# Projections of a cross-attention in a fixed order of TensorE, with a split first load and two products of zeros ahead

## The chip, the core and the metric

The kernel runs on one core of a Trainium2 chip. The core has a matrix engine (TensorE, PE in the profile; its weight loads are listed as PEld), a vector engine (VectorE, DVE), an engine for activations (ScalarE, ACT), GpSimd (POOL), and SyncE (SP), whose queue issues nearly all DMAs of this kernel. Work is held in SBUF, products come out in PSUM (eight banks), inputs, outputs and stored intermediates lie in DRAM. The metric is the time of one execution on the device in microseconds (us); three runs of the kernel before gave a median of 2944.82.

## What is computed

Two blocks of a gated network on x (8 batches, 512 rows, 256 columns). The change touches the first part of the first block, a cross-attention of x with a context, with 16 heads of 64:

```python
q = layernorm(x) @ Wq.T + bq          # 512 x 1024 for each batch
k = ctx @ Wk.T + bk
v = ctx @ Wv.T + bv
gate = relu(box_embedding(boxes) @ Wg.T + bg)      # 512 x 512 for each head
att = softmax(log(max(gate, 1e-6)) + q k.T / sqrt(64))
x1 = x + tanh(g_xattn) * (att v @ Wo.T + bo)
```

The kernel takes the gate, with its floor of 1e-6, as a factor on exp of the scores. After it come an attention over the batch, a mixture of eight experts, a second cross-attention and a spiking feed-forward layer, which stay as they are. All is 32-bit floating point.

## The kernel before, in words

`gated_cross_attention` (L273) has two stages. The **projection stage** (L371 to L406) computes keys, values and queries of all eight batches, stores them to DRAM (`kdr`, `vdr`, `qdr` in the profile), and prepares the terms of the gate from the boxes. The **attention stage** (from L408) reads them back, for 32 blocks of 128 queries.

*The projections* (`project_all`, L177). The setup loads the bias `bk`, four pieces of the key weights `wk_` (256 KB each), and after the first piece batch 0's context `ctxT` (512 KB) and rows `xt` (512 KB); then `wv`, `bv`, `wq`, `bq`. VectorE scales `wq` and `bq` (L209, L210). `batch(b)` (L215) issues the loads of batch b+1, takes the statistics of `xt` (L60 to L63, in `Ctx.stats`; the power -0.5 is on GpSimd) and normalizes it in place (L68). Then come eight key tiles: `project` (L223) makes each as two 128x512 products over the two halves c of the 256 columns into a PSUM tile `pk`, and ScalarE adds the bias and writes it to an SBUF tile `st` (L230), which a DMA stores (L235). Each product shows as two PE instructions in the profile, so a tile is four. Eight value tiles follow in the same way into `pv`; VectorE adds the bias into `vs` (L245), stored once per batch (L251). Then `xt` is transposed by PE into `pt` and copied to `xnT` (L258, L261), and eight query tiles are made with `project` and stored (L264). PSUM has two buffers each of `pk`, `pv` and `pt`; `st` has four buffers, and a fifth tile waits until the store of the first has landed.

*The boxes* (`box_terms`, L85). At setup, key centres `kcs` are computed from a load `kc` and stored (L98 to L102, `kcd<-kcs`); sizes are turned into sines and cosines `tt` on ScalarE (L105 to L126); `tt` is put in another order (`tk`), transposed by PE in two pieces through one PSUM tile, copied to `tT` and stored (L129 to L140, `kxd<-tT`). Its `batch(b)` makes and stores `asb` (L154 to L172). In batches 1 to 5, `offsets` and `features` (L399 to L406) prepare the gate's inputs `emb` of the first query blocks on VectorE and ScalarE, with pieces of some 1.5 to 2.8 us each.

*Who sets the order.* In the projection stage nothing is fixed by hand: a planner (part of the language's compiler) puts the instructions of every engine, and the DMA issues of SP, in an order. It takes what it believes ready, the earlier in the code first. Every engine and SP's queue then run their lists strictly in that order. In the attention stage, PE, ScalarE and VectorE follow the order of the code (`manual_schedule`, L561), except for the first block's gate products (L557 to L560), which the planner places.

*The boundary.* The pools of the attention stage, `xbig` (gate tiles), `xwk` (loads, scores) and `xps` (PSUM), lie where the released pools of the projection stage lay. By default, whatever first uses such memory waits for all users of the released pools there. Its first instructions are the loads of `qT`, `kT` and `v` (L430, L419, L425), 20 gate halves (L449, copied by ScalarE and VectorE in turn, L455) and the first scores (L469).

*Before all this*, L1696 to L1699 load the two gates of the network into `tg` and take their Tanh.

Of the kernel before, what the change touches and what calls it, by code (L numbers as in the profile page):

```python
# [12 lines left out]
F32 = mybir.dt.float32  # L13
I32 = mybir.dt.int32
AF = mybir.ActivationFunctionType
ALU = mybir.AluOpType
# [4 lines left out]
P = 128  # L21
# [63 lines left out]
def box_terms(cx, a, d, es):  # L85
# [40 lines left out]
    )  # L126


    tk = wk.tile([P, 2, 8, NT // 2], F32, name="tk")  # L129
    for g in range(2):  # L130
        nc.vector.tensor_copy(
            tk[:, g], tt[:, g * NT // 2 : (g + 1) * NT // 2].rearrange("p t a c -> p (a c) t")
        )
        pt = ps.tile([P, P], F32, name="pt", tag="t")
        nc.tensor.transpose(pt, tk[:, g].rearrange("p j t -> p (j t)"), ident)
        tT = w2.tile([P, P], F32, name="tT", tag="tT")
        nc.vector.tensor_copy(tT, pt)
        nc.sync.dma_start(
            out=d["kx"][g, 0:8, :].rearrange("j (t p) -> (j t) p", p=P), in_=tT
        )  # L140
    one = wk.tile([B // 2, S], F32, name="one")
    nc.gpsimd.memset(one, 1.0)
    for g in range(2):
# [7 lines left out]
    neg = wm[:, 0, :, H : 2 * H]  # L151
    nc.vector.tensor_scalar(neg, neg, -1.0, None, ALU.mult)

    def batch(b):  # L154

        shape = [P, NQ, 4, 2 * H]
        parts = []
        for c in range(2):
            part = w2.tile(shape, F32, name=f"asb{c}", tag=f"asb{c}")
            nc.vector.tensor_tensor(  # L160
                part, wm[:, c].unsqueeze(1).to_broadcast(shape),
                tt[:, b * NQ : (b + 1) * NQ, :, c].unsqueeze(3).to_broadcast(shape), ALU.mult,
            )
            parts.append(part)
        asb = parts[0]
        nc.vector.tensor_tensor(asb, asb, parts[1], ALU.add)
        for t in range(NQ):
            r0 = (b * NQ + t) * P
            nc.sync.dma_start(
                out=d["qx"][:, r0 : r0 + P, :].rearrange("j p h -> p j h"),  # L170
                in_=asb[:, t].rearrange("p a (c h) -> p (a c) h", h=H),
            )  # L172
# [1 line left out]
    return batch  # L174


def project_all(cx, a, d, wp):  # L177

    tc, nc, ident = cx.tc, cx.nc, cx.ident
    wk = wp.enter_context(tc.tile_pool(name="qw", bufs=1))  # L180
# [1 line left out]
    ps = wp.enter_context(tc.tile_pool(name="qps", bufs=2, space=PSUM))  # L182
    ctxTs, xts = {}, {}

    def load(b):
        ctxTs[b] = w2.tile([P, 2, S], F32, name="ctxT", tag="ctxT")
        nc.sync.dma_start(out=ctxTs[b], in_=a["ctxT"][b])
        xts[b] = w2.tile([P, NQ, D], F32, name="xt", tag="xt")
        nc.sync.dma_start(
            out=xts[b], in_=a["x"][b * S : (b + 1) * S, :].rearrange("(t p) d -> p t d", p=P)  # L190
        )

    wk_ = wk.tile([P, 2, H * DK], F32, name="wk_")
    bk = wk.tile([P, PAIRS], F32, name="bk")
    nc.sync.dma_start(out=bk, in_=a["bk"])
    for m in range(4):
        cols = slice(m * 2 * P, (m + 1) * 2 * P)
        nc.sync.dma_start(out=wk_[:, :, cols], in_=a["wkT"][:, :, cols])
        if m == 0:
            load(0)  # L200
    wv = wk.tile([P, 2, H * DK], F32, name="wv")
    nc.sync.dma_start(out=wv, in_=a["wvT"])
    bv = cx.bcast(wk, a["bv"], "bv")
# [8 lines left out]
    for v in vs:  # L212
        nc.gpsimd.memset(v[:, :, :, :, DK : DK + 1], 1.0)

    def batch(b):  # L215
        if b + 1 < B:
            load(b + 1)
        ctxT, xt = ctxTs.pop(b), xts.pop(b)
        mv, rs = cx.stats(w2, xt, NQ)
        xn = xt  # L220
        cx.normalize(xn, xt, mv, rs, NQ)

        def project(w, bias, src, name, m):  # L223
            pk = ps.tile([P, S], F32, name="pk", tag="p")
            for c in range(2):
                nc.tensor.matmul(  # L226
                    pk, w[:, c, m * P : (m + 1) * P], src[:, c, :], start=(c == 0), stop=(c == 1)
                )
            st = w2.tile([P, S], F32, name="st", tag="st", bufs=4)
            nc.scalar.activation(st, pk, AF.Identity, bias=bias[:, m : m + 1])  # L230
            return st

        for m in range(PAIRS):
            st = project(wk_, bk, ctxT, "k", m)
            nc.sync.dma_start(out=d["k"][b, m], in_=st)  # L235
        v = vs[b % 2]
        for kc in range(NQ):
            for n in range(2):
                pv = ps.tile([P, 512], F32, name="pv", tag="v")
                for c in range(2):  # L240
                    nc.tensor.matmul(  # L241
                        pv, ctxT[:, c, kc * P : (kc + 1) * P], wv[:, c, n * 512 : (n + 1) * 512],
                        start=(c == 0), stop=(c == 1),
                    )
                nc.vector.tensor_tensor(  # L245
                    v[:, 4 * n : 4 * n + 4, kc, :, 0:DK],
                    pv.rearrange("p (a t d) -> p a t d", t=2, d=DK),
                    bv[:, n * 512 : (n + 1) * 512].rearrange("p (a t d) -> p a t d", t=2, d=DK),
                    ALU.add,
                )  # L250
        nc.sync.dma_start(  # L251
            out=d["v"][b].rearrange("a p k -> p a k"), in_=v.rearrange("p a k t d -> p a (k t d)")
        )
        xnT = w2.tile([P, 2, S], F32, name="xnT", tag="xnT")
        for c in range(2):
            pt = ps.tile([P, S], F32, name="pt", tag="t")
            for t in range(NQ):
                nc.tensor.transpose(  # L258
                    pt[:, t * P : (t + 1) * P], xn[:, t, c * P : (c + 1) * P], ident
                )  # L260
            nc.vector.tensor_copy(xnT[:, c, :], pt)  # L261
        for m in range(PAIRS):
            st = project(wq, bq, xnT, "q", m)
            nc.sync.dma_start(  # L264
                out=d["q"][b * NQ : (b + 1) * NQ, :, m, :].rearrange("t p q -> p t q"),
                in_=st.rearrange("p (t q) -> p t q", q=P),
            )
        return xnT

    return batch  # L270


def gated_cross_attention(cx, a, tg, x1q, d, front):  # L273

# [3 lines left out]
    with ExitStack() as es:  # L280
# [16 lines left out]
        def load_keys(b):  # L297
            for r0 in (0, 2 * QB, 64, 64 + 2 * QB):
                nc.sync.dma_start(
                    out=kd[r0 : r0 + 2 * QB, b % 2, :],  # L300
                    in_=d["kc"][2 * b + (1 if r0 % 64 else 0)].partition_broadcast(2 * QB),
                )
# [63 lines left out]
        def features(j, *fns):  # L366
            for fn in fns:
                if 0 <= j < NSTEP:
                    fn(j)

        with ExitStack() as pro:  # L371
            batch = project_all(cx, a, d, pro)
            bp = pro.enter_context(tc.tile_pool(name="bq", bufs=1))
            box = box_terms(cx, a, d, pro)
            bx = bp.tile([P, NSTEP * NP, 2], F32, name="bx")
# [4 lines left out]
            nc.vector.tensor_tensor(qi, bx[:, :, 1], bx[:, :, 0], ALU.subtract)  # L380
            nc.vector.tensor_scalar(qi, qi, 1.0, None, ALU.add)
            nc.vector.reciprocal(qi, qi)
            for b in range(B):
                xnT = batch(b)
                box(b)
                if b == 0:
                    load_keys(0)

                if b < 4:
                    w, cols = wst[b // 2], slice(b % 2 * 8 * P, (b % 2 + 1) * 8 * P)  # L390
                    nc.gpsimd.tensor_copy(w[0:1, cols][:, 0:1], xnT[0:1, 0, 0:1])
                    nc.sync.dma_start(out=w[0:GR, cols], in_=a["wst"][:, cols])
                if b in (4, 5):
                    w = wo[:, 4 * (b - 4) : 4 * (b - 3), :]
                    nc.gpsimd.tensor_copy(w[0:1, 0, 0:1], xnT[0:1, 0, 0:1])
                    nc.sync.dma_start(out=w, in_=a["woT"][:, 4 * (b - 4) : 4 * (b - 3), :])
                if b == 6:
                    bo = cx.bcast(cp, a["bo"], "bo")
                if b in (1, 3, 5):  # L399
                    j = b // 2  # L400
                    offsets(j, 0, NP)
                    features(j, sizes, clip, log)
                if b in (2, 4):
                    j = b // 2 - 1
                    load_products(j)
                    features(j, turns, whole, rest, rest_sizes, sines, place)  # L406

        front(-1)  # L408
        big = es.enter_context(tc.tile_pool(name="xbig", bufs=2))
        wk = es.enter_context(tc.tile_pool(name="xwk", bufs=2))  # L410
        ps = es.enter_context(tc.tile_pool(name="xps", bufs=1, space=PSUM))
        gates, qTs, xts, kTs, vTs = {}, {}, {}, {}, {}
        es_, ats, pos, oTs = {}, {}, {}, {}

# [1273 lines left out]
def flamingo_gated_block(ctx: ExitStack, tc: tile.TileContext, a, out):  # L1688
# [4 lines left out]


    tg = const.tile([P, 5], F32, name="tg")
    nc.sync.dma_start(out=tg[:, 0:2], in_=a["g_xattn"].partition_broadcast(P))  # L1696
    nc.sync.dma_start(out=tg[:, 2:4], in_=a["g_ffn"].partition_broadcast(P))
    nc.scalar.activation(tg[:, 0:4], tg[:, 0:4], AF.Tanh)
    nc.vector.tensor_scalar(tg[:, 4:5], tg[:, 3:4], 0.2, None, ALU.mult)  # L1699

    x1q = [dram.tile([B * P, D], F32, name=f"x1q{q}") for q in range(NQ)]
    y1d = dram.tile([NT * P, D], F32, name="y1d")
# [33 lines left out]
            j = slice(2 * k - 10, 2 * k - 8)  # L1736
            cx.normalize(xf0[:, j], xf0[:, j], mv[:, j], rs[:, j], 2)

    gated_cross_attention(cx, a, tg, x1q, d, front)

    lp = ctx.enter_context(tc.tile_pool(name="late", bufs=1))
    moe = ctx.enter_context(tc.tile_pool(name="moe", bufs=1))
# [146 lines left out]
```

## Time and profile before

| what | value |
|---|---|
| runs of the kernel before | 2944.82 us median (2941.93 to 2946.64) |
| the profiled execution | 2944.38 us, its span 2942.6 us |
| PE busy over the span | 2887.5 us (98%), 15308 matmul instructions |
| DVE, ACT, POOL busy | 1826.0, 1411.9, 138.6 us |
| first PE instruction | 7.52 us |
| last projection product | run of 32 query instructions from 340.06 us |
| first gate product (L449) | 354.90 us |
| first scores (L469) | 363.02 us |
| 7.52 to 363.00 us | PE busy 347.69, DVE 126.74, ACT 121.86 of 355.48 us; DMA share 0.70 |

How to read it: the span runs from the first to the last instruction of the execution. A timeline row gives the start, the duration, the engine, the line of the code, the output and the inputs, the number of instructions merged in it, and in brackets how long the engine had been idle before it and what ended the wait. "SPq" rows are DMA issues on SP's queue. Matmuls are pipelined and their ends are modelled, so PE is read by the starts of its instructions and by its idle times rather than by its busy share.

### The profile page before, as it was taken

What the parts mean: (1) busy time and instruction counts of PE and PEld (TensorE: products, weight loads), DVE (VectorE), ACT (ScalarE), POOL (GpSimd) and SP (SyncE); (2) the same over time, 40 slices, a digit from 0 to 9 for tenths busy, and PEclk for the clock granted to TensorE, in tenths of its full rate; (3) what the DMA queues carried; (4) which work ended last, traced back from release to release, by engine and by line L of the source; (5) the groups of instructions that cost most, each with busy time, mean ns of one, the idle gap of its engine ahead of it and who ended that gap; (6) DMA issues with size and microseconds to landing.
All of it is one profiled execution on the core that took longest, in us unless ns stands there. A gap on an engine that the chain in (4) does not pass through costs nothing.

```text
span 2942.6 us, 39447 instructions
## 1 busy us (share of the span) xinstructions
PE 2887.5 (98%) x15308; PEld 2114.9 (72%) x15308; DVE 1826.0 (62%) x2862; ACT 1411.9 (48%) x2212; POOL 138.6 (5%) x138
## 2 busy tenths in 40 slices
PE   8999999999999999999999999999999999999998
PEld 3444478888888888888888888877776666456566
DVE  6432177777777777777777778557862012566758
ACT  4332256566666666656565665425542112343434
POOL 2000000000000000000000000000002111212100
PEclk9999999999999999999999999999999999999999
DMA  7775545555555555554646464543124432211000
GB/s 226 220 232 182 180 119 154 143 153 144 148 154 143 156 141 159 135 163 131 166 133 168 128 166 129 138 135 129 49 58 138 149 127 93 93 43 58 29 15 22
DMA packets 269338, 386.05 MB, mean 131 GB/s; under 512 B 55304, under 2 KB 133000, under 8 KB 266336
## 3 DMA queue, kind: packets, MB, share of 16 engines
q1 hardware_dynamic: 266080, 375.15, 44.0%
q0 software_dynamic: 3072, 8.39, 1.0%
q8 instruction: 121, 1.98, 0.3%
q14 instruction: 65, 0.53, 0.1%
HBM read 237.23 MB, written 78.07 MB: 107 GB/s over the span
## 4 chain that ended last, share of the span: by engine, by line
PE 79%; DVE 13%; DMA 2%; issue 2%; ACT 1%; SPq 1%; POOL 0%; ACTq 0%; DVEq 0%; POOLq 0%
PE pg L449 13%; PE po L505 11%; PE pS L469 7%; PE pk L226 6%; PE pT L485 6%; PE ph L1535 4%; PE pw L536 4%; PE ph L1320 4%; PE py L1329 4%; PE py L1550 4%; PE pv L241 3%; DVE nm L473 2%; PE pz L1507 2%; DVE lt L346 2%; PE pq L700 2%
## 5 line engine op out<-in xcount | busy, mean ns | idle before, releaser
L476 ACT ACTIVATE e<-pS,nm 128x512 f32<-128x512 f32 x512 | 323.8, 683 | 577.7 <-DVE nm L473 577.1
L449 PE MATMUL pg<-wst,emb 116*128 116x208 f32 (+1 forms) x2560 | 582.5, 351 | 8.1 <-DVE gate L455 5.8
L449 PEld LDWEIGHTS pg<-wst,emb 116*128 116x128 f32 x2560 | 414.7, 190 | 205.9 <-issue 81.2
L505 PEld LDWEIGHTS po<-v,at 128*128 128x128 f32 x4096 | 493.0, 192 | 0.1
L505 PE MATMUL po<-v,at 128*128 128x65 f32 x4096 | 485.7, 272 | 0.0
L473 DVE TENSOR_REDUCE nm<-pS 128x2 f32<-128x1024 f32 x256 | 312.6, 1221 | 176.4 <-PE pS L469 176.4
L487 DVE SCALAR_TENSOR_TENSOR at<-gate,pT 128x1024 f32<-128x1024 f32 x256 | 311.2, 1215 | 47.1 <-PE pT L485 46.1
L469 PE MATMUL pS<-kT,qT 64*128 64x512 f32 x1024 | 292.3, 643 | 5.1 <-ACT e L476 2.0
L485 PE MATMUL pT<-ident,e 128*128 128x128 f32 x2048 | 266.5, 273 | 0.0
L485 PEld LDWEIGHTS pT<-ident,e 128*128 128x128 f32 x2048 | 239.8, 141 | 14.0 <-DVE o L513 1.5
L455 DVE COPY gate<-pg 128x416 f32<-128x416 f32 (+1 forms) x289 | 164.7, 570 | 51.4 <-PE pg L449 31.1
L455 ACT COPY gate<-pg 128x416 f32<-128x416 f32 x351 | 166.5, 530 | 34.1 <-PE pg L449 31.7
L1333 DVE TENSOR_TENSOR ye<-py,b 128x256 f32<-128x256 f32 x32 | 13.6, 424 | 208.0 <-PE py L1329 208.0
L1324 ACT ACTIVATE hT<-ph,eb 128x512 f32<-128x512 f32 x64 | 44.0, 687 | 174.9 <-PE ph L1320 174.9
L226 PE MATMUL pk<-ctxT,wk__129 128*128 128x512 f32 x256 | 114.8, 604 | 10.3 <-DMA ctxT<-in_ctxT 7.5
L63 POOL TENSOR_TENSOR ln_rs<-ln_ve,mhalf 128x4 f32<-128x4 f32 (+1 forms) x25 | 25.4, 1017 | 2049.4 <-DVE ln_ve L62 1989.2
L1535 PE MATMUL ph<-xnT,wf 128*128 128x512 f32 (+2 forms) x320 | 118.7, 513 | 1.8 <-ACT xnT L1405 1.8
L536 PE MATMUL pw<-wo,oT 128*128 128x256 f32 x512 | 117.6, 383 | 0.5 <-ACT oT L528 0.5
L241 PE MATMUL pv<-wv,ctxT 128*128 128x512 f32 x256 | 114.7, 594 | 1.2 <-DVE vs L245 1.1
L469 PEld LDWEIGHTS pS<-kT,qT 64*128 64x128 f32 x1024 | 78.2, 185 | 50.5 <-issue 36.5
L1320 PE MATMUL ph<-dT,w 128*128 128x512 f32 x256 | 111.9, 595 | 2.4 <-DVE dT L1305 2.4
L226 PE MATMUL pk<-xnT,wq 128*128 128x512 f32 x256 | 112.8, 594 | 0.6 <-DVE xnT L261 0.6
(259 smaller groups left out, 3959.8 us busy)
## 6 DMA issues: line engine op xcount, KB each, us to landing
v<-vdr SPq DMA_DIRECT2D x256, 260.0 KB
kT<-kdr SPq DMA_DIRECT2D x256, 256.0 KB
emb<-lt SPq DMA_DIRECT2D x64, 520.0 KB
emb<-nt SPq DMA_DIRECT2D x64, 520.0 KB
vdr<-vs SPq DMA_DIRECT2D x8, 2080.0 KB
kdr<-st SPq DMA_DIRECT2D x64, 256.0 KB
qdr<-st SPq DMA_DIRECT2D x64, 256.0 KB
qT<-qdr SPq DMA_DIRECT2D x32, 512.0 KB
```

Of the source, the lines that this page charges most:

```text
L226: nc.tensor.matmul(pk, w[:, c, m * P : (m + 1) * P], src[:, c, :], start=(c == 0), stop=(c == 1))
L449: nc.tensor.matmul(pg[:, c, 0 : nq * H], embs[i % 2][R, blk // 2, blk % 2, kc * P : (kc + 1) * P], wst[i % 2][R, q0 * H : (q0 + nq) * H], ...
L455: copy(gates[i][:, :, 2 * hf : 2 * hf + 2, q0 : q0 + nq].rearrange("p h k q -> p k h q"), pg[:, :, 0 : nq * H].rearrange("p k (q h) -> p k ...
L469: nc.tensor.matmul(pS[:, t, :], qTs[i][rows, p, :], kT[rows, :], start=True, stop=True)
L473: nc.vector.tensor_reduce(nm, pS, AX.X, ALU.max, negate=True)
L476: nc.scalar.activation(e[:, t, :], pS[:, t, :], AF.Exp, bias=nm[:, t : t + 1])
L485: nc.tensor.transpose(pT[:, t, kc, :], e[:, t, kc * P : (kc + 1) * P], ident)
L487: nc.vector.scalar_tensor_tensor(at, gates[i][:, 2 * p : 2 * p + 2], 1e-6, pT, ALU.max, ALU.mult)
L505: nc.tensor.matmul(po[:, 2 * (p % 2) + t, :], at[:, t, kc, :], v[:, kc, t, :], start=(kc == 0), stop=(kc == NQ - 1),)
L536: nc.tensor.matmul(pw, oT[:, c, :], wo[:, c, :], start=(c == 0), stop=(c == PAIRS - 1))
L1320: nc.tensor.matmul(ph, w1[:, c, f * P : (f + 1) * P], dT[:, c, :], start=(c == 0), stop=(c == 1),)
L1535: nc.tensor.matmul(ph[:, 0:n], wf[:, c, f * P : (f + 1) * P], xnT[:, c, tok], start=(c == 0), stop=(c == 1),)
```

## The change

The diff, cut to its core ("..." where lines are left out):

```diff
 def box_terms(cx, a, d, es):
-    tk = wk.tile([P, 2, 8, NT // 2], F32, name="tk")
-    for g in range(2):
-        ...
+    def rows():
+        tk = wk.tile([P, 2, 8, NT // 2], F32, name="tk")
+        for g in range(2):
+            nc.vector.tensor_copy(tk[:, g], tt[...])
+            pt = ps.tile([P, P], F32, name="pt", tag="t")
+            nc.tensor.transpose(pt, tk[:, g].rearrange("p j t -> p (j t)"), ident)
+            tT = w2.tile([P, P], F32, name="tT", tag="tT")
+            nc.vector.tensor_copy(tT, pt)
+            nc.sync.dma_start(out=d["kx"][g, 0:8, :]..., in_=tT)
     def batch(b):
+        if b == 0:
+            rows()
...
-def project_all(cx, a, d, wp):
+def project_all(cx, a, d, wp, load_gates):
-    def load(b):
-        ...
+    def load(b, keys=True, queries=True):
+        if keys:
+            ctxTs[b] = w2.tile([P, 2, S], F32, name="ctxT", tag="ctxT")
+            for c in (slice(0, 1), slice(1, 2)) if b == 0 else (slice(0, 2),):
+                nc.sync.dma_start(out=ctxTs[b][:, c, :], in_=a["ctxT"][b][:, c, :])
+                if c.start == 0 and b == 0:
+                    load_keys(0)
+        if queries:
+            xts[b] = ...
+    zero = w2.tile([P, S], F32, name="st", tag="st", bufs=4)
+    nc.vector.memset(zero, 0.0)
+    for _ in range(2):
+        nc.tensor.matmul(
+            ps.tile([P, S], F32, name="pk", tag="p", bufs=3), zero[:, 0:P], zero, start=True, stop=True
+        )
     wk_ = wk.tile([P, 2, H * DK], F32, name="wk_")
+    load(0, queries=False)
+    load_gates()
     bk = wk.tile([P, PAIRS], F32, name="bk")
     nc.sync.dma_start(out=bk, in_=a["bk"])
-    for m in range(4):
-        ...
+    for m in range(1, 4):
+        load_keys(m)
+    load(0, keys=False)
...
+    def project(w, bias, src, m):
+        pk = ps.tile([P, S], F32, name="pk", tag="p", bufs=3)
+        ...
+    def value(b, m):
+        kc, n = divmod(m, 2)
+        pv = ps.tile([P, 512], F32, name="pv", tag="v", bufs=3)
+        ...
+        if m == PAIRS - 1:
+            nc.sync.dma_start(out=d["v"][b]..., in_=v...)
+    def turn(b):
+        xnT = xnTs[b] = w2.tile([P, 2, S], F32, name="xnT", tag="xnT")
+        for c in range(2):
+            pt = ps.tile([P, S], F32, name="pt", tag="t", bufs=1)
+            ...
+            yield
     def batch(b):
         if b + 1 < B:
             load(b + 1)
+        normed(b)
+        turns = turn(b)
+        if b == 0:
+            for m in range(PAIRS):
+                key(b, m)
+        for m in range(PAIRS):
+            if b:
+                key(b, m)
+            value(b, m)
+            if b:
+                query(b - 1, m)
+            if m > PAIRS - 3:
+                next(turns)
+        if b == B - 1:
+            for m in range(PAIRS):
+                query(b, m)
+        return xnTs[b]
...
-            for b in range(B):
-                ...
+            with tc.manual_schedule(engines={mybir.EngineType.PE}):
+                for b in range(B):
+                    ...
-        big = es.enter_context(tc.tile_pool(name="xbig", bufs=2))
-        wk = es.enter_context(tc.tile_pool(name="xwk", bufs=2))
-        ps = es.enter_context(tc.tile_pool(name="xps", bufs=1, space=PSUM))
+        big = es.enter_context(tc.tile_pool(name="xbig", bufs=2, reuse_waits="tile"))
+        wk = es.enter_context(tc.tile_pool(name="xwk", bufs=2, reuse_waits="tile"))
+        ps = es.enter_context(tc.tile_pool(name="xps", bufs=1, space=PSUM, reuse_waits="tile"))
...
-    nc.sync.dma_start(out=tg[:, 0:2], in_=a["g_xattn"].partition_broadcast(P))
-    ...
+    def load_gates():
+        nc.sync.dma_start(out=tg[:, 0:2], in_=a["g_xattn"].partition_broadcast(P))
+        ...
```

In words: (1) Batch 0's context is loaded in two halves of 256 KB, the first piece of `wk_` between them, and these are the first loads of all; the loads of the gates and of `bk` follow, then the rest of `wk_`, and then `xt`. (2) Ahead of the first key, PE multiplies a tile of zeros by itself twice; the products take two of the `pk` buffers and the zeros one of the four `st` buffers. (3) `pk`, which keys and queries share, and `pv` have three PSUM buffers each, and the `pt` of `project_all` one; with the one of `box_terms` that makes eight banks. (4) In the batch loop PE runs in the order of the code. Batch 0 makes its eight keys, then its eight values; the later batches take in turn one key tile, one value tile and one query tile of the batch before; `xt` is transposed in two steps, behind the seventh and the eighth turn; the last batch's queries follow at the end. (5) `rows()`, the two transposes of `tk` with their stores, is called in the first `batch` of `box_terms`, behind batch 0's products. (6) The three pools of the attention stage are asked to wait tile by tile: a tile waits for the tiles that it overlies, and not for the whole of the released pools.

## The prediction

> **What bounds the kernel now.** The page's chain of work that ended last says whose time the span is made of:
>
> ```profile
> PE 79%; DVE 13%; DMA 2%; issue 2%; ACT 1%; SPq 1%; POOL 0%; ACTq 0%; DVEq 0%; POOLq 0%
> ```
>
> So a microsecond taken from PE's idle time, or added to it, is a microsecond of the span, unless a later wait eats it. The change touches the first 363 us (projections, and the entry to the attention stage), so I read PE's timeline there next. The columns are start, duration, engine, line, out<-in, count, and in brackets the idle time before it:
>
> ```profile
> 7.52 12.87 PE L226 MATMUL pk<-ctxT,wk__129 128*128 128x512 f32 x24 [7.52 <-DMA ctxT<-in_ctxT]
> ...
> 30.66 3.60 PE L226 MATMUL pk<-ctxT,wk__129 128*128 128x512 f32 x8
> ...
> 61.63 3.70 PE L226 MATMUL pk<-ctxT,wk__129 128*128 128x512 f32 x8 [1.05 <-ACT st L230]
> ...
> 68.97 7.17 PE L226 MATMUL pk<-ctxT,wk__129 128*128 128x512 f32 x16 [1.06 <-ACT st L230]
> ...
> 205.22 7.13 PE L241 MATMUL pv<-wv,ctxT 128*128 128x512 f32 x16 [1.08 <-DVE vs L245]
> ...
> 354.90 1.65 PE L449 MATMUL pg<-wst,emb 116*128 116x208 f32 x8 [0.87 <-issue]
> 357.80 4.12 PE L449 MATMUL pg<-wst,emb 116*128 116x208 f32 x20 [1.25 <-ACT gate L455]
> 363.02 1.09 PE L469 MATMUL pS<-kT,qT 64*128 64x512 f32 x2 [1.10 <-issue]
> ```
>
> Four PE instructions make one tile of keys, values or queries. A run of 32 (227.66 us) takes 13.90, of which 0.17 is the last one's tail: 0.429 each, 1.72 a tile. PE loses 7.52 before it starts; 2.40 in the first run (12.87 - 0.17 - 24 x 0.429); 4.49 in five waits (1.05, 1.06, 1.08, and 0.70 at 189.90, 0.60 at 340.06); 3.22 at the stage boundary (0.87, 1.25, 1.10). That is all a change here can win, some 17.6 us.
>
> Note the order in batch 0: six key tiles first, keys 7 and 8 only at 30.66, after value tiles. The timelines of ACT, SP's queue and DVE tell why:
>
> ```profile
> 16.99 0.69 ACT L230 ACTIVATE st<-pk,bk 128x512 f32<-128x512 f32 x1 [1.03 <-PE pk L226]
> ...
> 28.78 1.35 ACT L230 ACTIVATE st<-pk,bk 128x512 f32<-128x512 f32 x2 [2.18 <-DMA kdr<-st]
> ```
> ```profile
> 15.00 0.36 SPq L376 DMA_DIRECT2D bx<-in_boxq  x1
> 21.27 0.33 SPq L102 DMA_DIRECT2D kcd<-kcs  x1
> ...
> 22.57 0.43 SPq L189 DMA_DIRECT2D xt<-in_x  x1
> 23.11 2.54 SPq L235 DMA_DIRECT2D kdr<-st  x4
> ```
> ```profile
> 17.91 1.23 DVE L209 TENSOR_SCALAR wq<-wq 128x2048 f32<-128x2048 f32 x1 [4.72 <-DMA wq<-in_wqT]
> ```
>
> Four st tiles exist. ACT fills them by 17.7, and the fifth waits until 28.78 for the first key store to land. That store stands in SP's queue behind kcd<-kcs (21.27), whose DVE input stands behind the scaling of wq, which waits for wq until 17.91. Today PE fills the hole with values.
>
> **The change, part by part.** (Minus is gain.)
>
> *Start.* The first load that PE needs is issued at 2.11 now, and at 0.72 (the place of the tg loads) after: 1.39 earlier. Only 512 KB instead of 768 must be there; 256 KB at the 340 GB/s that the DMA view shows at 6 to 8 us is 0.77. PE's first real product comes at 7.52 - 2.16 = 5.36; its second half (another 0.77) is there before the two c=0 instructions (0.86) end. **-2.2** (-1.4 with the shift alone, to -3). The tg loads and the Tanh follow later; nothing reads tg before L542. bk moves too, but lands before the first key ends.
>
> *Zeros.* In the first run the weight loads start 0.85 apart, and 0.43 apart from about 12.3, 4.8 us after PE began:
>
> ```profile
> 10.21 0.34 PEld L226 LDWEIGHTS pk<-ctxT,wk__129 128*128 128x128 f32 x1 [0.52 <-issue]
> ...
> 13.36 0.19 PEld L226 LDWEIGHTS pk<-ctxT,wk__129 128*128 128x128 f32 x1 [0.24 <-issue]
> ```
>
> The granted clock reads 1.00 in both stretches, so that column does not show this; the pitch does. Two zero products are four instructions, 3.4 us at the slow pitch, behind a memset (no row of DVE; POOL's 128x1024 takes 0.94), so from about 1.2 to 4.6, before data arrives. They serve 3.4 of the 4.8 slow microseconds; the 1.4 left cost 0.7. **-1.7** (0 to -2.4). The trace shows no zero operands.
>
> The Trainium skill ("TensorE: Matmul & The Clock Gate", Part 1, "What's actually happening") says that a busy window of about 3.4 us frees the clock and an idle window of that length halves it again. By the first half the zeros would win all 2.4; by the second the change is exposed wherever its fixed order leaves PE idle.
>
> *Three banks and interleaved turns.* Keys and queries share three pk tiles instead of two, and in batches 1 to 7 come once per 2.57 us instead of 1.72. A late ACT, DVE or store is covered longer, so I let the five waits (4.49) go and put back 0.5: **-4.0** (0 to -4.5). In the last batch, query 0's c=0 product (0.86) hides the copy of xnT's second half, which costs 0.60 now.
>
> *Boundary.* With waits by tile, the first gate copies (357.20) need not wait for the last query store. But pg may lie on a bank that the last query's ACT reads, and kT/qT are loaded at 357.19 now and may still wait. Half of 3.22: **-1.6** (0 to -3.2).
>
> *rows().* It moves behind batch 0's products, and PE's order is fixed there: the second transpose waits for the copy of the first out of the one pt tile. Before that copy DVE may have the last value add (0.69), xnT's copy (0.68), then tT (0.28): **+1.3** (0 to +2). Now, values hide it (28.72 to 29.80). Its two stores leave SP later, and load_products, their reader, comes in batch 2.
>
> *Key 8 of batch 0.* The fixed order has eight keys ahead of the first value. Four st and three pk tiles take seven; the eighth waits until ACT empties a pk, hence for the first store to land. Seven keys end at 5.36 + 0.7 + 7 x 1.72 = 18.1. When does the store land? SP's view shows an issue waiting for the landing of the one eight places ahead (bx for bv, kcd for wq), and the loads that follow crow are ready at any time and come first in the code, so the store stays behind them. Load bytes ahead of wq are the same, starting 1.4 earlier: wq at 16.5. From there to kcd it is 3.36 now (17.91 to 21.27), to kdr 1.84 more, to ACT 5.67 more, 0.74 for ACT: 28.1; if DVE leaves out the three xt rows (1.05), 27.0. I take 27.6: PE idles **+9.5**. Nothing else stands in its order; DVE, ACT and SP do their box work in this time and don't win from it later. If the planner puts kcd behind the stores: SP waits for wq (16.5), three loads (1.5), 5.67, 0.74 = 24.4, a stall of 6.3. Lower end 0, should the stores go out ahead of the loads; upper end 11.
>
> *Slow pitch after the gap.* A gap of 2.46 us is followed by 0.85 pitches in this trace:
>
> ```profile
> 2499.58 2.17 PE L1402 MATMUL pt<-ident,xn 128*128 128x128 f32 x8 [2.46 <-DVE xn L1390]
> ```
>
> Its eight transposes take 2.0 instead of 0.87, and the three weight loads after them stand 0.85 apart: 1.1 + 3 x 0.43 = 2.4 lost. **+2.4** (0 to +2.4) for a gap of 6 to 9.
>
> **Sum:** -2.2 - 1.7 - 4.0 - 1.6 + 1.3 + 9.5 + 2.4 = +3.7. The profiled execution took 2944.38 (span 2942.6, 1.8 around it), 0.4 below the median of the runs. 2944.4 + 3.7 = **2948.1**. In the attention stage PE's order is kept, and I count nothing there.
>
> **Rivals.**
> - *No stall:* the planner lets the first stores out before the loads, or they land by 18. The terms 9.5 and 2.4 go: 2944.4 - 8.2 = 2936.2. For it: SP's order is planned anew. Against it: in the trace the loads come first though st was full from 12.0 on.
> - *A short stall* (kcd behind the stores, 6.3): 2944.4 + 0.5 = 2944.9. For it: kcd's place hangs on when kcs is thought ready. Against it: kc's load and SP's row before it keep their distance.
> - *Slower through the stores in every batch:* key and query stores in SP's one queue stand behind a waiting vdr<-vs store or an asb store (vdr waits on DVE up to 12.4 us now), and PE can no longer take values instead. If batches 1 to 7 each lose what batch 1 lost at 61.63 and 68.97 (2.1), it is 14.8 instead of the 0.5 counted: 2948.1 + 14.3 = 2962.4. It decides from a store that leaves more than two turns late (four st tiles: 10.3 us) with the three pk tiles (some 7 us) used up. Against it: that cover is larger than the longest wait seen.
> - *The change not doing what it says* is part of the above: zeros that warm nothing and waits by tile that find the same tile are the upper ends of their terms.
>
> **How the numbers follow.** About 0.2% (5.9 us) is what a measurement can tell from no change. Forecast 0.5 (own range 2943 to 2953), no stall 0.2, short stall 0.2, slower through stores 0.1. Faster than 2938.9: 0.8 of the no-stall case, 0.15 of the short one, a little of the forecast: 0.22. Slower than 2950.7: the fourth case and 0.3 of the forecast: 0.25. Within: 0.53. The range leaves out half of the no-stall case's lower side and the fourth case: 2934.5 to 2954.
>
> **What would show it.** Right: PE's first real product near 5.4, with weight loads already 0.43 apart within three of them; a gap of 6 to 11 before the last four key instructions of batch 0, whose releaser is ACT st, ACT's own wait there being kdr<-st; slow pitches after it; no wait over 0.3 in batches 2 to 7; the first gate copy within 2 us of the last query's ACT. Wrong: kdr<-st in SP's queue ahead of ctxT of batch 1; no gap near 18; PE waits on ACT st in several batches.

## The result, and the profile after

The kernel after takes 2949.02 us in the median of 16 runs (2945.64 to 2952.23), the kernel before, run beside it, 2943.28 us (2938.98 to 2950.47, 16 runs). The ratio is 1.0019, 95% interval 1.0012 to 1.0026: 0.2% slower, and inside the predicted range. The profiled execution of after took 2947.74 us, its span 2946.0, so 3.4 us more than that of before (2944.38 and 2942.6).

Where do the 3.4 us come from? The first scores start at 366.62 us instead of 363.02, 3.60 later. From there to the end of the span it is 2579.4 us, and 2579.6 before: in these two executions all of the difference arises ahead of the first scores, as the prediction assumed. The chain of work that ended last is still PE's (its line on the page of after):

```profile
PE 80%; DVE 13%; DMA 2%; issue 2%; SPq 1%; ACT 1%; POOL 0%; DVEq 0%; ACTq 0%; POOLq 0%
```

PE's timeline in after, in the columns of the prediction (start, duration, engine, line, out<-in, count, idle time before it and what ended it):

```profile
1.44 3.78 PE L211 MATMUL pk<-st 128*128 128x512 f32 x4 [1.44 <-DVE st L209]
5.01 3.81 PE L241 MATMUL pk<-ctxT,wk__131 128*128 128x512 f32 x8
9.29 8.82 PE L241 MATMUL pk<-ctxT,wk__131 128*128 128x512 f32 x20 [0.47 <-DMA wk__131<-in_wkT]
30.43 3.78 PE L241 MATMUL pk<-ctxT,wk__131 128*128 128x512 f32 x4 [12.31 <-ACT st L245]
...
51.19 0.33 PE L149 MATMUL pt<-ident,tk 128*128 128x128 f32 x1 [1.23 <-DVE tT L151]
...
345.91 14.09 PE L241 MATMUL pk<-xnT,wq 128*128 128x512 f32 x32
360.87 5.82 PE L499 MATMUL pg<-wst,emb 116*128 116x208 f32 x28 [0.87 <-issue]
366.62 1.12 PE L519 MATMUL pS<-kT,qT 64*128 64x512 f32 x2
```

Read it from the top. The zeros run from 1.44, and the first real product starts at 5.01 instead of 7.52. Seven keys (28 instructions) end near 18.1. Then comes the hole of 12.31 us before the four instructions of key 8, with ACT's `st` as releaser. After the wait at 51.19 no row of PE has a bracket until the first gate product: the timeline shows no wait of PE in batches 1 to 7.

The other engines in the hole (SP's queue, then ACT, then DVE):

```profile
22.01 0.33 SPq L102 DMA_DIRECT2D kcd<-kcs  x1
22.38 0.42 SPq L426 DMA_DIRECT2D crow<-in_crow  x1
22.84 0.43 SPq L194 DMA_DIRECT2D ctxT<-in_ctxT  x1
23.32 0.43 SPq L199 DMA_DIRECT2D xt<-in_x  x1
23.85 2.27 SPq L250 DMA_DIRECT2D kdr<-st  x4
```
```profile
29.69 1.96 ACT L245 ACTIVATE st<-pk,bk 128x512 f32<-128x512 f32 x3 [3.83 <-DMA kdr<-st]
```
```profile
18.65 1.23 DVE L230 TENSOR_SCALAR wq<-wq 128x2048 f32<-128x2048 f32 x1 [3.08 <-DMA wq<-in_wqT]
```

From bottom to top this is the chain: `wq` has landed at 18.65, DVE's scaling of it stands ahead of `kcs`, the store of `kcs` (22.01) stands ahead of the first key stores in SP's queue (23.85), and ACT gets a free `st` at 29.69.

### The profile page after: what moved, and what is told of

Same layout as the page of the kernel before. It is cut to its first block, busy times and chain, and to the rows that moved or that the text cites. A ratio compares the mean times of both kernels' runs of the same rounds, so it can differ in the third digit from the quotient of the medians.

```text
span 2946.0 us, 39450 instructions
## 1 busy us (share of the span) xinstructions
PE 2886.1 (98%) x15312; PEld 2114.0 (72%) x15312; DVE 1827.1 (62%) x2863; ACT 1413.1 (48%) x2212; POOL 139.0 (5%) x138
## 4 chain that ended last, share of the span: by engine, by line
PE 80%; DVE 13%; DMA 2%; issue 2%; SPq 1%; ACT 1%; POOL 0%; DVEq 0%; ACTq 0%; POOLq 0%
PE pg L499 12%; PE po L555 11%; PE pk L241 7%; PE pS L519 7%; PE pT L535 5%; PE ph L1585 4%; PE ph L1370 4%; PE pw L586 4%; PE py L1379 4%; PE py L1600 4%; PE pv L264 3%; DVE nm L523 2%; PE pz L1557 2%; PE pS L1534 2%; PE pq L750 2%
## 5 line engine op out<-in xcount | busy, mean ns | idle before, releaser
L241 PE MATMUL pk<-ctxT,wk__131 128*128 128x512 f32 x256 | 121.7, 601 | 12.8 <-ACT st L245 12.3
L268 DVE TENSOR_TENSOR vs<-pv,bv 128x512 f32<-128x512 f32 x64 | 44.1, 689 | 144.5 <-PE pv L264 144.5
L241 PE MATMUL pk<-xnT,wq 128*128 128x512 f32 x256 | 119.3, 592 | 0.0
```

The lines of the kernel that those rows point to most:

```text
L241: nc.tensor.matmul(pk, w[:, c, m * P : (m + 1) * P], src[:, c, :], start=(c == 0), stop=(c == 1))
```

## The experiments

The theory: key 8 of batch 0 waits in PE's fixed order for the first key store, because four `st` tiles are in use and the store stands late in SP's queue. Between its first product and the first scores, no other wait of PE in after is longer than 1.23 us. The ratios are to the kernel before in the same call, with 95% intervals; "first scores" is the start of the first scores product in the profiled execution (363.02 before, 366.62 after).

**1. Key 8 last.** Batch 0 makes seven keys, its values with both steps of `turn`, and then key 8.

```diff
-            for m in range(PAIRS):
+            for m in range(PAIRS - 1):
                 key(b, m)
...
+        if b == 0:
+            key(b, PAIRS - 1)
         if b == B - 1:
```

> The changed kernel with batch 0's eighth key made after its values; nothing else moves. Theory (the eighth key waits for the first key store, and values can fill that time): the gap of 12.3 us and the slow pitch after it (2.8) go; the first gate product, at 360.9 us in the changed kernel and 354.9 before, comes at 345.5 to 347; the time is 0.9965 to 0.9975 of the kernel before. Rival (the hole only moves: values wait for their VectorE adds, which stand behind the scaling of wq until 22 us): 2 to 6 us of new waits on VectorE among batch 0's values, first gate product at 348 to 352, 0.998 to 0.999.

Measured: 2937.2 us, ratio 0.9980 (0.9971 to 0.9989), first scores at 356.67, so 9.95 earlier than after. The hole in batch 0 is gone, but not all of its 12.31 us and the slow pitch behind it come back. Batch 1 has a new wait; PE's timeline, and ACT's below it:

```profile
57.65 3.52 PE L241 MATMUL pk<-xnT,wq 128*128 128x512 f32 x4 [2.89 <-ACT st L245]
61.88 1.98 PE L241 MATMUL pk<-ctxT,wk__131 128*128 128x512 f32 x4 [0.71 <-ACT st L245]
```
```profile
56.91 0.69 ACT L245 ACTIVATE st<-pk,bk 128x512 f32<-128x512 f32 x1 [4.03 <-DMA kdr<-st]
57.62 1.28 ACT L387 ACT_TABLE_LOAD   x1
58.91 2.34 ACT L387 ACTIVATE lt<-lt 116x2560 f32<-116x2560 f32 x1
```

It is the same mechanism, one batch later: an `st` tile not yet stored (4.03), and behind it in ACT's order a table load and a logarithm (3.6 us) that keep the next `st` waiting too. In after, batch 1 has no such wait; that the hole had given the stores time to drain fits this, but no run shows it by itself. The first gate product comes at 350.92, so the theory's 345.5 to 347 was missed. The time is in the rival's range, but not for its cause: the values of batch 0 wait for DVE only once, for 0.30 us.

**2. A fifth `st` tile.** PE's order is that of after. To make room, the tile `one` of the boxes takes the buffer of `asb0`.

```diff
-    one = wk.tile([B // 2, S], F32, name="one")
+    one = w2.tile([B // 2, S], F32, name="one", tag="asb0")
-    zero = w2.tile([P, S], F32, name="st", tag="st", bufs=4)
+    zero = w2.tile([P, S], F32, name="st", tag="st", bufs=5)
-        st = w2.tile([P, S], F32, name="st", tag="st", bufs=4)
+        st = w2.tile([P, S], F32, name="st", tag="st", bufs=5)
```

> The changed kernel with five st tiles instead of four, and the tile of ones, for room, in one of asb's buffers; PE's order stays. With five st tiles ScalarE can empty the fifth key without any store landing, so the eighth key finds a free bank. Theory (the store of the first key is what holds PE): no gap before the eighth key, first gate product at 345.5 to 347. Rival (ScalarE itself is held, by its box work between 22 and 26 us, or its order puts the fifth key behind it): the gap stays, or ends near 23 us instead of 30.4.

Measured: 2932.3 us, ratio 0.9959 (0.9943 to 0.9975), first scores at 353.73. PE's timeline:

```profile
5.02 14.49 PE L241 MATMUL pk<-ctxT,wk__131 128*128 128x512 f32 x32
...
36.11 0.33 PE L149 MATMUL pt<-ident,tk 128*128 128x128 f32 x1 [1.34 <-DVE tT L151]
...
61.09 1.98 PE L241 MATMUL pk<-xnT,wq 128*128 128x512 f32 x4 [0.53 <-ACT st L245]
...
353.73 1.09 PE L519 MATMUL pS<-kT,qT 64*128 64x512 f32 x2 [1.20 <-DMA kT<-kdr]
```

All 32 key instructions of batch 0 stand in one run: five `st` and three `pk` tiles take eight keys. The stores leave SP no earlier (25.03), yet no key of batch 0 waits for them. The order of PE is unchanged. Up to the last queries 14.20 us come back (they start at 331.71 instead of 345.91), up to the first scores 12.89: the entry to the attention stage, with its wait of 1.20 for `kT`, keeps the rest. The first gate product, at 346.71, is where the theory had it.

**3. Key stores on another queue.** Batch 0's key stores are issued by ScalarE.

```diff
-        nc.sync.dma_start(out=d["k"][b, m], in_=st)
+        (nc.sync if b else nc.scalar).dma_start(out=d["k"][b, m], in_=st)
```

> The changed kernel with batch 0's key stores issued from ScalarE's queue instead of SP's; their tiles, sizes and PE's order stay. Theory (the first store lands late because it stands in SP's queue behind kcd<-kcs and the loads of batch 1): it is issued near 8 us and lands before 18, no gap before the eighth key, first gate product at 345.5 to 347.5. Rival (the DMA engines are full of loads until wq lands at 18.6, and a store lands only after them): a gap of 1 to 4 us remains, first gate product at 348 to 351. If both are wrong the gap stays at 12.

Measured in a single execution: 2937.41 us, span 2935.6, first scores at 355.00. ACT's timeline:

```profile
7.55 0.67 ACT L245 ACTIVATE st<-pk,bk 128x512 f32<-128x512 f32 x1
8.26 0.35 ACTq L250 DMA_DIRECT2D kdr<-st  x1
...
16.05 0.69 ACT L245 ACTIVATE st<-pk,bk 128x512 f32<-128x512 f32 x1 [3.03 <-DMA kdr<-st]
```

The first store leaves at 8.26 instead of 23.85, the fifth `st` is free at 16.05 instead of 29.69, and key 8 does not wait. With four `st` tiles and the same PE order only the queue of these stores differs. So the hole needs both, four tiles and the late place in SP's queue: taking away either removes it. A smaller price remains: 1.85 us in the values of batch 0, 1.34 at `rows()`, and 1.71 for an `st` tile at 142.68. With it the first gate product (349.25) misses the theory's 345.5 to 347.5.

**4 and 5. Without the zeros**, alone, and with key 8 last. Both leave out an addition of the change, no part of the result.

```diff
-    zero = w2.tile([P, S], F32, name="st", tag="st", bufs=4)
-    nc.vector.memset(zero, 0.0)
-    for _ in range(2):
-        nc.tensor.matmul(...)
```

> The changed kernel without the two products of zeros. Theory (PE's restart at 30.4 us hangs on loads, SP and VectorE, not on when the first seven keys end): seven keys end 2 us later, the gap is 2 us shorter, the restart stays at 30.4 and the first gate product at 360.9 within 0.4. Rival (every microsecond at the start is one of the span): first gate product at 362.9 to 363.4.

> The kernel with the eighth key last, and without the two products of zeros. Theory (they take the slow pitch of the first 4.8 us of work off the real products, and nothing hides that once the gap is gone): 1.7 to 2.5 us later at the first gate product than with them, 0.0006 to 0.0009 of the time. Rival (the wait for the second piece of the key weights at 9.3 us, 0.5 now, and other waits of batch 0 take it up): under 1 us later.

Measured: 2947.23 us, ratio 1.0012 (1.0003 to 1.0022), first scores at 366.24, alone; 2937.71 us, 0.9986 (0.9976 to 0.9996), 357.31, with key 8 last. In the first, the run of seven keys ends at 19.4 instead of 18.1, and the hole before key 8 shrinks to 11.69. PE restarts at 31.07, 11.8 us after DVE began to scale `wq` (19.25), and in after it is 11.8 us too (30.43 and 18.65): the restart hangs on `wq` and not on the end of the keys, so the hole takes what the zeros buy.

With key 8 last, the last queries start 1.51 us later without the zeros (337.46 against 335.95). Of this, 1.1 us comes from the keys; batch 0 takes half of it back, and a longer wait in batch 1 (4.79 instead of 2.89 and 0.71) adds about 1 us. The entry then gives about 1 us back: without the zeros, in runs 4, 5 and 12, the first gate product does not wait (0.88 in run 1, 0.17 more with the tail). Why the zeros bring this wait is not shown. So 0.47 us is left there, and 0.64 at the first scores. The number is the rival's (under 1 us); its cause, other waits of batch 0, explains only a part.

**6. The waits by tile alone**, as the only change to the kernel before.

```diff
-tc.tile_pool(name="xbig", bufs=2)
+tc.tile_pool(name="xbig", bufs=2, reuse_waits="tile")
...
```

> The kernel before with the three pools of the attention stage waiting tile by tile, and nothing else of the change. Theory (the change's gain at the boundary, 2.4 us between the last queries and the first scores, is of this part alone): the wait of 1.25 us on the first gate copies and most of the 1.1 before the first scores go, 0.87 before the first gate product stays; first scores at 360.5 to 361 instead of 363.0, 0.9992 of the time before. Rival (the first scores wait for the loads of keys that wait for the last query stores): first scores within 0.5 of 363.

Measured: 2945.48 us, ratio 1.0009 (1.0000 to 1.0018), first scores at 361.96. Of the three waits at the boundary two are gone (0.87, which was expected to stay, and 1.25), but the scores now wait 1.35 for `kT`. The first scores come 1.06 earlier, half of what was expected. The last queries start 0.71 later than before (340.77), with a new wait of 0.53 ahead of them, so the boundary itself gains 1.77; in after it gains 2.25. In the total the two readings disagree: the profiled execution took 2942.77, 1.6 less than that of before, the median is 2.7 more than that of before. The boundary's share is read from the trace; the total stays open.

**7. The hole filled.** 13 products of zeros stand before key 8, in the `pv` banks, to keep PE busy; `zero` has its own tile. They compute nothing that is used.

```diff
+                if m == PAIRS - 1:
+                    for _ in range(13):
+                        nc.tensor.matmul(ps.tile(..., name="pv", tag="v", bufs=3),
+                            zero[:, 0:P], zero, start=True, stop=True)
                 key(b, m)
```

> The changed kernel with 13 more products of zeros (11.2 us) in the gap, ahead of the eighth key, into value banks; the zeros have a tile of their own, and the tile of ones lies in one of asb's buffers. Theory (the slow pitch after the gap comes of PE's idleness, as at the start): weight loads 0.43 us apart from the eighth key on, restart near 30.4 as now, first gate product 2.4 to 2.8 us earlier than 360.9. Rival (the slow pitch comes of something else at that time, such as traffic): it stays.

Measured: 2948.71 us, ratio 1.0017 (1.0007 to 1.0026), first scores at 367.73. The weight loads behind the hole, first in after, then with the hole filled (restarts at 30.43 and 31.33):

```profile
31.45 0.34 PEld L241 LDWEIGHTS pk<-ctxT,wk__131 128*128 128x128 f32 x1 [0.52 <-issue]
32.30 0.34 PEld L241 LDWEIGHTS pk<-ctxT,wk__131 128*128 128x128 f32 x1 [0.52 <-issue]
...
36.36 0.19 PEld L264 LDWEIGHTS pv<-wv,ctxT 128*128 128x128 f32 x1 [0.31 <-issue]
36.79 0.19 PEld L264 LDWEIGHTS pv<-wv,ctxT 128*128 128x128 f32 x1 [0.24 <-issue]
```
```profile
31.86 0.19 PEld L241 LDWEIGHTS pk<-ctxT,wk__131 128*128 128x128 f32 x1 [0.24 <-issue]
32.29 0.19 PEld L241 LDWEIGHTS pk<-ctxT,wk__131 128*128 128x128 f32 x1 [0.24 <-issue]
```

So the slow pitch follows from PE's idleness: loads 0.85 apart in after, 0.43 when filled. The granted clock of after says the same; it is the third number from the end of each row, behind the stretch and the busy times of the engines:

```profile
18.20:22.40 4.20, 0.00 (x0) 0.00 (x0) 3.75 (x11) 0.27 (x2) 0.00 (x0) 1.00 0.07 25
22.60:30.40 7.80, 0.00 (x0) 0.00 (x0) 6.43 (x21) 3.93 (x7) 0.00 (x0) 0.50 0.83 252
30.50:36.10 5.60, 5.60 (x7) 2.46 (x8) 4.02 (x12) 1.84 (x3) 1.39 (x1) 0.50 0.97 240
36.20:40.00 3.80, 3.80 (x10) 1.71 (x9) 2.97 (x5) 0.00 (x0) 0.00 (x0) 1.00 0.71 126
```

It falls to 0.50 some 4.4 us after PE went idle (18.11) and stays there until 36.1, 5.7 us after the restart. In run 7 it reads 1.00 from 31 to 36 us. From the restart to the ninth load it is 5.93 in after and 3.11 filled: 2.8 us. The total shows none of it, since `wq` landed 0.94 later in this run (19.59), the wait of `rows()` grew from 1.23 to 2.73, and after that gap the pitch was slow for some instructions (about 1.2 us).

**8. The scaling of `wq` later.** Its two lines stand behind batch 0's values in the code.

```diff
-    nc.vector.tensor_scalar(wq, wq, 1.0 / math.sqrt(DK), None, ALU.mult)
-    nc.vector.tensor_scalar(bq, bq, 1.0 / math.sqrt(DK), None, ALU.mult)
...
+        if b == 0:
+            (the same two lines)
         if b == B - 1:
```

> The changed kernel with the scaling of wq and bq on VectorE written behind batch 0's values instead of in the setup. Theory (kcd<-kcs, and the key stores behind it, wait for kcs, which stands on VectorE behind that scaling): kcd is issued near 18.7 instead of 22.0, when the DMA eight places ahead lands, the restart comes near 27.1 instead of 30.4 and the first gate product 3 to 3.5 us earlier than 360.9. Rival (SP is held by the landing of wq alone or by kc): kcd and the restart stay.

Measured in a single execution: 2946.96 us, first scores at 365.69. The planner still put the scaling of `wq` ahead of `kcs`; of the long pieces only the three `xt` rows (1.05) left their place between the two: they now run ahead of the scaling, while DVE waits for `wq`. `kcd` left at 21.14, 2.31 after `wq` landed (18.83) instead of 3.36, and the hole ended 1.0 earlier. So the edit did not do what it was meant to, and the expected 3.3 stays untried; the part that did move agrees with the chain.

**9. The planner's order.** The change without the fixed order of PE in the projection stage.

```diff
-            with tc.manual_schedule(engines={mybir.EngineType.PE}):
+            if True:
                 for b in range(B):
```

> The changed kernel with PE's order in the projection stage left to the planner; loads, zeros, banks, turns and waits by tile stay. Theory (of all parts only the fixed order costs time, and only at batch 0's eighth key): the planner puts values ahead of it, there is no gap over 2 us, first gate product at 345 to 348, 0.9965 to 0.998 of the kernel before. Rival (three banks and turns need the fixed order, since the planner's order gave waits of 1 us in batches 1, 4 and 7 before): waits of 3 us or more in later batches, first gate product at 349 or later.

Measured: 2934.6 us, ratio 0.9972 (0.9963 to 0.9982), first scores at 352.55. The first gate product, at 346.80, is where the theory had it, and no wait of PE is over 2 us. The planner makes seven keys, then values, then key 8, and PE waits 0.45 for it:

```profile
5.02 12.75 PE L241 MATMUL pk<-ctxT,wk__131 128*128 128x512 f32 x28
...
30.97 1.98 PE L241 MATMUL pk<-ctxT,wk__131 128*128 128x512 f32 x4 [0.45 <-ACT st L245]
```

In batch 1 two waits for `st` remain (1.02 and 0.35); the 3 us of the rival do not come.

**10. Key 8 last, and the two halves of `rows()` apart**, one in batch 0 and one in batch 1.

```diff
-        if b == 0:
-            rows()
+        if b < 2:
+            rows(b)
```

> The kernel with the eighth key last, and rows() called for one half in batch 0 and for the other in batch 1, so that the second transpose does not wait for the copy of the first. Theory: the wait of 1.2 us before the second transpose goes, 1.2 to 1.5 us earlier at the first gate product than with the eighth key last alone; 0.996 to 0.997 of the kernel before, the fastest of all. Rival (the first transpose or its store waits elsewhere now): no difference.

Measured: 2936.62 us, ratio 0.9978 (0.9968 to 0.9988), first scores at 357.28. The wait of `rows()` is gone, and the wait in batch 1 is 4.16 instead of 2.89: nothing is won over run 1, as the rival had it.

**11. Five `st` tiles and `rows()` apart** (the edits of 2 and 10).

> Five st tiles, and the two halves of rows() apart, one in batch 0 and one in batch 1, so that no transpose of tk waits for the copy of the one before. With five st tiles alone PE lost 1.34 us at rows() and 0.53 us in batch 1. Theory: the 1.34 goes, and, as no long gap is near, the 0.53 in batch 1 does not take it back: first scores at 352.4 (353.73 with five st tiles alone), ratio to the kernel before 0.9955. Rival: as with key 8 last, the later wait for a store takes it back (0.53 grows to 1.9), first scores at 353.7, ratio 0.996.

Measured: 2932.56 us, ratio 0.9965 (0.9951 to 0.9978), first scores at 352.65, against 353.73 with five tiles alone. The last queries start 1.85 earlier than there (329.86), but the entry takes part of it back:

```profile
352.65 1.38 PE L519 MATMUL pS<-kT,qT 64*128 64x512 f32 x2 [1.97 <-DMA kT<-kdr]
353.96 3.02 PE L499 MATMUL pg<-wst,emb 116*128 116x208 f32 x8
```

The scores wait for the load of `kT` (1.97 instead of 1.20), and eight gate products behind that gap take 3.02 us instead of 1.67, so that the gate products after the second pair of scores start at 357.97, 0.56 later than in run 2. The intervals of the two overlap; nothing is shown to be won. The first scores come close to where the theory had them (352.4), the ratio does not.

**12. Five `st` tiles without the zeros** (the edits of 2 and 4).

> Five st tiles, and the two products of zeros left out (an addition of the change, no part of the result). Without zeros in the changed kernel nothing was lost, since the gap before key 8 took it all. Theory: where there is no gap the zeros are worth the slow pitch that they replace, 1.7 to 2.4 us: first scores at 355.4 to 356.2, some 2 us longer than five st tiles with zeros, ratio 0.9968. Rival: other waits behind them (the second piece of the key weights, 0.47; rows(), 1.34; batch 1, 0.53) take most of it: first scores at 354.3 or earlier, ratio as with zeros.

Measured: 2933.42 us, ratio 0.9970 (0.9960 to 0.9980), first scores at 352.71. The keys end 1.0 us later than with zeros, and the last queries still start 1.08 later (332.79 against 331.71); at the entry the first gate product no longer waits for ACT and the scores wait 0.26 for `kT` instead of 1.20, and all of it is given back. The theory (2 us for the zeros) fell; by these profiles they are worth 1.1 us as far as the last queries and nothing beyond, and the intervals overlap. So the rival's number came (under 354.3), but what takes the gain back stands at the entry and not among the waits that it named.

Five `st` tiles, the least edit that empties the hole, gives the lowest ratio of all: 0.4% below the kernel before, where the change as made is 0.2% above it. Its interval overlaps those of runs 9, 11 and 12, so these four are not told apart.

## Why the prediction was right

Right: the time (2948.1 predicted, 2949.02 measured), the hole with its place and chain, and that it swallows the gains. Several terms were off, and their errors nearly cancel. All times below are from the traces of before and after.

- *Start*, -2.2: it was 7.52 - 5.01 = -2.51.
- *Zeros*, -1.7: the weight loads are 0.43 apart from 5.65 on, and the first run loses 0.2 instead of 2.40. So -2.2 at this place. But PE then came too early for the second piece of `wk_` and waited 0.47 at 9.29, 0.64 with the tail of the run before it. That wait was not foreseen. Runs 4, 5 and 12 show that none or little of this reaches the end.
- *Three banks and turns*, -4.0: five waits of 4.49 us went and nothing was put back. The term was too small by about 3. A wait also costs the modelled tail of the run before it (0.17 each, 0.85), and some 1.7 us of before is neither in its waits nor in the slow start: the 736 products (0.429 each) and the transposes ahead of the last queries are 323.1 us of work, and PE took 332.54 from its first product to there. So about -7.0, and the prediction's list of what a change can win (17.6) was short by 2.5.
- *Boundary*, -1.6: the last queries start 5.85 later than before, the first scores 3.60 later, so -2.25. The waits of 1.25 and 1.10 went, the 0.87 stayed: the first gate product starts 0.09 after the last query's ACT ends (360.78), which fits the shared bank that the prediction named; no run shows the bank itself. The first gate copy came at 361.98, 1.2 after the last query's ACT, as listed.
- *rows()*, +1.3: 1.23, from the second copy of `tT`.
- *Key 8*, +9.5: 12.31, or 12.5 with the tail. Every link had its predicted length but one: `kcd` 3.36 after `wq`, `kdr` 1.84 later, ACT 5.84 (5.67), PE 0.74. The term was mis-sized by 3, and the step behind it is "load bytes ahead of wq are the same, starting 1.4 earlier: wq at 16.5". The use of `wq` began at 18.65, later than before (17.91). SP's queue shows why: the first load leaves at 0.72 in both kernels, and the split context is one issue more, so the load of `wq` is issued at 7.52 instead of 7.08. What was moved ahead was only the order, not the number of issues: the small loads of the gates and of `bk`, first before, now stand behind the first three (2.52 to 3.9 us). The DMA share is 0.68 from 4 to 6 us and 0.70 from 6 to 8, where it was 1.03 and 0.97, and by 8 us both kernels have moved some 1.3 MB (worked out from the GB/s of the 2 us stretches): the early start had won no bytes. From 8 to 18 us the share is 0.93 to 1.09 in both. The other 0.6 is from taking 27.6, halfway to a variant in which DVE left out the `xt` rows; it did not.
- *Slow pitch*, +2.4: 2.8, by run 7. The size was partly luck: in the row that it was taken from, the clock reads 0.50 from 2500.6 to 2503.9, some 3.4 us, which costs 1.7 at most, and the transposes there also waited for DVE's `xn`. The prediction set the granted clock aside because it reads 1.00 at the start; behind gaps the column does show the slow pitch.

The measured sum is -2.51 - 2.2 + 0.64 - 7.0 + 12.5 + 2.8 + 1.4 (rows with its tail) - 2.25 = +3.4, beside +3.60 read directly at the first scores, and +3.7 predicted. The hole was 3 us worse and the removed waits 3 us better than the prediction had them: right in mechanism, and partly lucky in the total.

The rivals: "a short stall" had `kcd` behind the key stores; `kcd` (22.01) leaves ahead of them (23.85), so its condition did not come. "No stall" is what runs 2 and 9 show when the hole is taken away (2932.3 and 2934.6; the rival's price was 2936.2). "Slower through the stores in every batch" did not come: batches 1 to 7 have no wait in after. But its mechanism, PE waiting for an `st` tile, shows in batch 1 in all runs in which the hole is gone and the key stores stay in SP's queue: 2.89 to 4.79 us in runs 1, 5 and 10, and 0.53 to 1.43 in runs 2, 9, 11 and 12.

What stays open: the medians of after and before differ by 5.7 us, the profiled executions by 3.4, and the prediction had 3.7. The profiled execution of before lies 1.1 above its median, that of after 1.3 below. In the runs with several executions the difference of the medians and that of the first scores agree within 2.3 us, except in run 6 (+2.7 and -1.06). A part of the scatter goes with the granted clock: of 80 runs of the kernel before, made beside the experiments, the four with a mean clock of 0.990 took 2947.6 to 2948.6 us and the 24 with 0.993 took 2936.9 to 2945.1. After reads 0.989 to 0.991 in all 16 runs, but the hole alone, with its 13.7 us at 0.50, takes 0.002 off its mean. So no trace here decides whether the waits by tile cost something that one profiled execution does not show.

## What to carry to other kernels

Before an engine's order is fixed, count for each of its instructions how many buffers the chain behind it needs until the first one comes free, and follow that buffer's release through every queue on its way: here one tile of 256 KB more was worth 0.6% of the kernel. An order that a planner found may be hiding such a wait, as values hid it before. And a gain ahead of a wait is no gain until the wait is gone: taking the zeros out and parting `rows()` mostly changed the length of a later wait.

## What the runs showed of the hardware

*The clock after a gap.* PE ran at the slow pitch, with a granted clock of 0.50, behind waits of 12.31 (after), 4.79 (run 5), 4.16 (run 10), 2.89 (run 1), 2.73 (run 7) and 1.97 us (run 11, eight gate products in 3.02 instead of 1.67). In before the clock reads 0.50 from 401.4 to 404.7, behind a wait of 1.54 us (before scores products at 401.28). It stayed at 1.00 after 2.33 (run 7) and 1.85 (run 3). So in these runs no single length decides between 1.5 and 2.4 us. The stretches at 0.50 last 3.4 us (runs 1, 5, 7 and 11), 6.8 (run 10) or 13.7 (after); in run 11 the clock falls only at 353.3, 0.7 after PE had started again. The Trainium skill ("TensorE: Matmul & The Clock Gate", Part 1, "What's actually happening") gives an idle window of about 3.4 us for the fall of the clock. Gaps of 1.54 to 2.89 us were enough here, so that length is no safe bound for a gap; the measurement decides.

*Where the column does not help.* In before the granted clock reads 1.00 from 7.5 to 12 us, while the weight loads stand 0.85 apart. At the start of the execution only the distance of the loads shows the slow pitch.

*Zeros count as work.* Two products of a tile of zeros (four instructions, 3.4 us at the slow pitch) put the first real products to the fast pitch from 5.65 us on, and 13 of them held it through the hole. In run 2 the same zeros left one more slow load (5.97), in run 11 none.

*Loads at the start.* Between 2 and 8 us SP issues one DMA per 0.4 to 0.7 us. With three small loads among them the DMA engines were not full in after (share 0.68 and 0.70 from 4 to 8 us); from 8 to 18 us they were (0.99 to 1.09, at 328 to 399 GB/s). The load of `wq` was issued at 7.08 before and at 7.51 to 7.56 in all runs with the split load on SP's queue alone, whatever they did later, and its scaling, where DVE stood waiting for it, began between 18.65 and 19.84: 11 to 12 us from issue to use, and 1.2 us apart in runs whose loads are alike. The end of the hole moves with it: 30.43 in after, 31.07 in run 4, 31.33 in run 7.
